# The last three of 39 expert blocks behind a test of the routing

## The chip, the cores and the metric

The kernel runs on one core of a Trainium2 chip. The core has five engines with an instruction stream each: TensorE (PE, matmuls; its weight loads are listed as PEld), VectorE (DVE), ScalarE (ACT), GpSimd (POOL) and SyncE (SP, which issues DMAs). They meet through semaphores. The metric is the device time of one execution in microseconds (us); lower is better. All data is float32.

## The reference

Two transformer-like layers on 8 sequences of 512 tokens with 256 features. In each layer the normalised input goes through a sequence mixer and a mixture of experts, and both results are added to the input. In the first layer the mixer is a state-space model in both directions, and the experts are these:

```python
logits = xt @ Wr + br                    # xt: 4096 tokens x 256, 8 experts
probs = softmax(logits)
gate = max(probs);  idx = argmax(probs)  # one expert for each token
h1 = maximum(xt @ W1[idx] + b1[idx], 0)  # 256 -> 1024
y = (h1 @ W2[idx] + b2[idx]) * gate      # 1024 -> 256
```

How many tokens an expert gets depends on the data. The second layer is an attention with 16 heads and a decay over the distance, and a mixture of experts with a fixed capacity; it needs the whole first layer of a sequence before it can begin on it.

## The kernel before, in words

**First layer, mixer.** The work is cut into 8 batches (one sequence each, 512 tokens) of 8 chunks (4 stretches of 128 tokens, each in two directions), 64 chunks in all. The order of every engine's instructions is written out by hand. A loop over the chunks issues, for each chunk, the state-space steps (`segments`, the exponentials of `cross`, `inside`, `before`, `pairs`, `behind`, `weigh`) and pieces of the neighbouring batches (`project`, `conv`, `z_part`, `output`). The first exponential of a chunk is on line 1111, the matmuls of `segments` on 1103, those of the projections on 915.

**Fills.** Between these the loop calls `fill(1)`, four times a chunk, five times in the first two chunks of a batch and in the last twelve chunks. One fill takes one step of a generator: first `rows`, which is `route0()` followed by `blocks()`, and when that has ended `rest`, which is `late()`. After the last chunk the steps of the last batch are issued with more fills between them, and what is left of `late` goes into the first steps of the second layer's attention.

**Routing.** `route0` (lines 472 to 528) finds the expert of each token and sorts the tokens into blocks of 128 of one expert each. An expert with n tokens gets n/128 blocks, rounded up. `end` holds the running sum of these, so its last entry is the number of blocks in use. In the worst case this is `NBLK` = (4096 + 8 x 127)/128, rounded down to 39, and the kernel always runs 39. A block behind the last one in use gathers rows of zeros, loads the weights of the last expert, and scatters its result to rows out of bounds, which are dropped.

**Blocks.** For each block GpSimd issues four indirect DMAs: a gather of the 128 token rows (`xd`, line 581), the two weight matrices of the expert (`w1`, `w2`, line 586, about 1 MB each), fetched up to two blocks ahead, and the scatter of the result (`put`, line 609). PE turns the rows (line 601), multiplies by `w1` (line 634) and `w2` (line 655); ScalarE and VectorE take half each of the activation (641, 643); ScalarE scales the bias (627) and VectorE combines (661). A block is five steps, so five fills.

**Late work.** `late` loads the second layer's weights into the space that the blocks' tiles leave (`second_weights`, lines 72 and 845 to 874; the release waits for the last scatter), and then runs, for each batch as its first layer is done, its normalisation (`norm`, lines 679 to 725), transposition and projections (`turn`, `project`, lines 737 to 744 and 246 to 280) and the second router (`route`, with matmuls on line 226). The three run side by side, one step of each in a fill.

The lines that set this order:

```python
rows, rest, sizes = itertools.chain(route0(), blocks()), late(), step_sizes()
...
def fill(n):
    for _ in range(n):
        if next(rows, "end") == "end":
            next(rest, None)
```

Of the kernel before, what the change touches and what calls it, by code (L numbers as in the profile page):

```python
# [32 lines left out]
NE, FF = 8, 1024  # L33
FC = FF // P
NBLK = (NT + NE * (P - 1)) // P
CAP = NT // NE
NE1 = NE - 1
NSLOT1 = NE1 * CAP
# [21 lines left out]
def tile_kernel(ctx: ExitStack, tc: tile.TileContext, t, out: bass.AP):  # L60
# [299 lines left out]
    number0 = l0c.tile([P, NBLK], I32, name="number0", tag="number0")  # L360
    ea = l0c.tile([P, 2 * NH], FP, name="ea", tag="ea")
    w_idx = l0c.tile([P, NBLK], I32, name="w_idx", tag="w_idx")

    dec_tok = l0c.tile([P, 2, NTILE, NH], FP, name="dec_tok", tag="dec_tok")

# [106 lines left out]
    def route0():  # L472

        big = r0b

        E3 = [P, NTILE, NE]
        pair0 = big.tile([P, NTILE, 2], FP, name="pair0", tag="pair0")
        G.iota(
            pair0[:, :, 0], pattern=[[P, NTILE]], base=1, channel_multiplier=1, allow_small_or_imprecise_dtypes=True
        )  # L480
        for pr in softmax_experts(big, proj[:, :, 2 * NH :], br):
            yield
        m, oh = first_max(big, pr, "a")
        V.tensor_copy(pair0[:, :, 1], m)
        yield
        rank, n = ranks(
            big, lambda name, shape: bank(name, shape, "e"), oh,
            lambda shape: row("rk_b").rearrange("p (a b) -> p a b", a=2),
        )
        yield  # L490
        over = big.tile([P, NE, NTILE], FP, name="over", tag="over")
        V.tensor_tensor(over, bc(n, 2, [P, NE, NTILE]), bc(iota_t, 1, [P, NE, NTILE]), ALU.is_gt)
        nb = big.tile([P, NE], FP, name="nb", tag="nb")
        V.tensor_reduce(nb, over, AX.X, ALU.add)
        end = big.tile([P, NE], FP, name="end", tag="end")
        V.tensor_copy(end, nb)
        for e in range(1, NE):
            V.tensor_tensor(end[:, e : e + 1], end[:, e : e + 1], end[:, e - 1 : e], ALU.add)
        yield
        first = big.tile([P, NE], FP, name="first", tag="first")  # L500
        V.tensor_tensor(first, end, nb, ALU.subtract)
        V.tensor_scalar(first, first, float(P), None, ALU.mult)
        V.tensor_tensor(rank, rank, bc(first, 1, E3), ALU.add)
        lo, hi = (big.tile([P, NTILE], FP, name=n, tag=n) for n in ("lc_l", "lc_h"))
        locate(big, slots_of(big, oh, rank, "a"), lo, hi)
        yield

        tp, n, entry = bank("tab", [P, NBLK, 2], "e"), TPB, None
        for i in range(0, NTILE + n, n):
            at = slice(i, i + n)  # L510
            ahead = entries(big, NBLK, lo[:, at], hi[:, at], pair0[:, at, :]) if i < NTILE else None
            if entry:
                enter(tp, entry, i == n, i == NTILE)
            entry = ahead
            yield
        V.tensor_copy(table0, tp)
        numbers(big, table0, number0)

        B3 = [P, NBLK, NE - 1]
        iota_b = big.tile([P, NBLK], FP, name="iota_b", tag="iota_b")  # L520
        G.iota(iota_b, pattern=[[1, NBLK]], base=0, channel_multiplier=0, allow_small_or_imprecise_dtypes=True)
        past = big.tile(B3, FP, name="past", tag="past")
        V.tensor_tensor(past, bc(end[:, : NE - 1], 1, B3), bc(iota_b, 2, B3), ALU.is_le)
        be = big.tile([P, NBLK], FP, name="be", tag="be")
        V.tensor_reduce(be, past, AX.X, ALU.add)
        V.tensor_scalar(be, be, float(P), pidx, ALU.mult, ALU.add)
        V.tensor_copy(w_idx, be)
        yield

    def decays():  # L530
# [33 lines left out]
    with ExitStack() as es:  # L564
# [9 lines left out]
        def fetch(j, *names):  # L574

            if j < NBLK:
                for name in names:
                    n, bufs = {"xd": (DM, 3), "w1": (KC * FF, 2), "w2": (FC * DM + FC + DM, 2)}[name]
                    w = held[name, j] = e2.tile([P, n], FP, name=name, tag=name, bufs=bufs)
                    if name == "xd":  # L580
                        G.indirect_dma_start(
                            out=w, out_offset=None, in_=xn0, bounds_check=NT + P - 1, oob_is_err=True,
                            in_offset=bass.IndirectOffsetOnAxis(ap=number0[:, j : j + 1], axis=0),
                        )
                    else:
                        G.indirect_dma_start(
                            out=w, out_offset=None, in_=t[name], bounds_check=NE * P - 1, oob_is_err=False,
                            in_offset=bass.IndirectOffsetOnAxis(ap=w_idx[:, j : j + 1], axis=0),
                        )
# [3 lines left out]
        def blocks():  # L593
            nonlocal e2
            r0.close()
            e2 = es.enter_context(tc.tile_pool(name="e2", bufs=2, side="right"))
            def turned(j):
                xd = held.pop(("xd", j))
                tp = bank("xdT_ps", [P, DM], "e")
                for k in range(KC):  # L600
                    T.transpose(tp[:, k * P : (k + 1) * P], xd[:, k * P : (k + 1) * P], ident)
                xdT = e2.tile([P, DM], FP, name="xdT", tag="xdT", bufs=3)
                A.copy(xdT, tp)
                return xdT

            sent = []

            def put(yo, number):
                one = G.indirect_dma_start(
                    out=yt0, out_offset=bass.IndirectOffsetOnAxis(ap=number, axis=0),  # L610
                    in_=yo, in_offset=None, bounds_check=NT - 1, oob_is_err=False,
                )
                for other in sent:
                    tc.declare_no_dep(one.ins, other.ins, reason="every token has one row")
                sent.append(one)

            made = None
            fetch(0, "xd", "w1", "w2")
            fetch(1, "xd", "w1", "w2")
            yield  # L620
            nxt = turned(0)
            yield
            for j in range(NBLK):
                xdT, (w1, w2) = nxt, (held.pop((name, j)) for name in ("w1", "w2"))
                b12 = w2[:, FC * DM :]
                yo = e2.tile([P, DM], FP, name="yo", tag="yo")
                A.mul(yo, b12[:, FC:], table0[:, j, 1:2])
                hT = [e2.tile([P, FC // 2, P], FP, name="hT", tag="hT", bufs=2) for _ in range(2)]
                for half in range(2):
                    hp = bank("h_ps", [P, FC // 2, P], "e")  # L630
                    for i in range(FC // 2):
                        f = half * FC // 2 + i
                        for k in range(KC):
                            T.matmul(  # L634
                                hp[:, i, :], w1[:, k * FF + f * P : k * FF + (f + 1) * P],
                                xdT[:, k * P : (k + 1) * P], start=(k == 0), stop=(k == KC - 1),
                            )
                    for i in range(FC // 2):
                        f = half * FC // 2 + i
                        if half == 0:  # L640
                            A.activation(hT[half][:, i, :], hp[:, i, :], AF.Relu, bias=b12[:, f : f + 1])
                        else:
                            V.tensor_scalar(hT[half][:, i, :], hp[:, i, :], b12[:, f : f + 1], 0.0, ALU.add, ALU.max)
                    if half == 0 and j:
                        put(*made)
                        fetch(j + 1, "w2")
                    if half == 0:
                        fetch(j + 2, "xd")
                    yield
                if j + 1 < NBLK:  # L650
                    nxt = turned(j + 1)
                    yield
                yp = bank("y_ps", [P, DM], "e")
                for f in range(FC):
                    T.matmul(  # L655
                        yp, hT[f // 4][:, f % 4, :], w2[:, f * DM : (f + 1) * DM], start=(f == 0), stop=(f == FC - 1)
                    )
                    if f == 3:
                        fetch(j + 2, "w1")
                        yield  # L660
                V.scalar_tensor_tensor(yo, yp, table0[:, j, 1:2], yo, ALU.mult, ALU.add)
                made = yo, number0[:, j : j + 1]
                yield
            put(*made)

        kept, turned = {}, set()

# [1173 lines left out]
```

## Time and profile before

| | |
|---|---|
| median of 3 runs | 2013.36 us (2012.37 to 2015.62) |
| the profiled execution | 2011.26 us |
| its span, first to last instruction | 2009.5 us |
| mean granted clock of TensorE | 0.943 of full speed |
| TensorE busy | 1818.5 us, 90% of the span |
| VectorE, ScalarE, GpSimd busy | 1459.0, 1176.2, 587.2 us |
| first and last block's closing VectorE step (line 661) | 220.4 and 878.4 us |
| first score matmul of the second layer (line 1533) | 1128.7 us |

The profile is of one execution. A group's line names the source line, the engine and operation, the tile written and those read, the shape, and the count; then busy us and mean ns of one, and then the time that the engine stood idle before these instructions, with what ended it. A matmul in float32 leaves two records for each call. "Issue" is time in which the engine waited for nothing that the profile shows. A row of busy time by stage gives each engine's busy us within a stretch of the span, then the granted clock of TensorE as a fraction and what the DMA engines did.

### The profile page before, as it was taken

Reading aid. Unit: us, or ns where it says so; the run is one execution under the profiler, and the core shown is the slowest. Engines: PE = TensorE matmul, PEld = TensorE weight load, DVE = VectorE, ACT = ScalarE, POOL = GpSimd, SP = SyncE. Lnnn points to the kernel's source line nnn. Section 1 sums busy time; section 2 is a strip of 40 time slices with the busy share of each in tenths; the row PEclk is TensorE's granted clock in tenths of the full one; section 3 lists DMA queues with packets and bytes.
Section 4 is the critical chain, followed back from the end, with each engine's and each line's share of the span. In section 5 each row is a group of like instructions: output and inputs, shape, how many; then the busy total and the mean of one; then the engine's idle time right before and its main releaser. Section 6 shows DMA issues by size and latency. Waiting matters only on the chain.

```text
span 2009.5 us, 33675 instructions
## 1 busy us (share of the span) xinstructions
PE 1818.5 (90%) x11956; PEld 1239.9 (62%) x11956; DVE 1459.0 (73%) x3344; ACT 1176.2 (59%) x2575; POOL 587.2 (29%) x528
## 2 busy tenths in 40 slices
PE   6566999899999999998898869999999999999997
PEld 6224677676767767664565546666666666666654
DVE  6587675767667576778557477878888878788885
ACT  4232454434545454454552337878887887788886
POOL 0042665655556574543330000101011111111030
PEclk8677999999999999998898679999999999999999
DMA  7010565545556554436553313222313222223171
GB/s 267 6 47 26 211 212 171 180 143 172 197 171 206 170 189 160 161 104 172 154 165 93 98 44 108 66 84 57 89 49 103 66 85 54 87 57 100 40 143 42
DMA packets 132967, 238.58 MB, mean 119 GB/s; under 512 B 20381, under 2 KB 94111, under 8 KB 120896
## 3 DMA queue, kind: packets, MB, share of 16 engines
q1 hardware_dynamic: 101952, 119.99, 19.1%
q0 software_dynamic: 29808, 115.78, 18.7%
q8 instruction: 96, 1.57, 0.3%
q10 hardware_dynamic: 1040, 0.66, 0.1%
q14 instruction: 71, 0.58, 0.1%
HBM read 183.58 MB, written 53.71 MB: 118 GB/s over the span
## 4 chain that ended last, share of the span: by engine, by line
PE 66%; DVE 14%; ACT 11%; issue 2%; DMA 1%; POOL 0%; SPq 0%; ACTq 0%; DVEq 0%; POOLq 0%
PE p_ps L1555 8%; PE h_ps L634 6%; PE pj L915 6%; PE y_ps L655 6%; ACT s L1548 6%; PE o_ps L1564 6%; PE s_ps L1533 4%; PE e_hp L1383 4%; PE e_yp L1396 4%; ACT pT L1556 3%; PE op L1060 3%; PE yd L1141 3%; PE seg L1103 2%; PE sp L1171 2%; PE yoff L1159 2%
## 5 line engine op out<-in xcount | busy, mean ns | idle before, releaser
L1538 DVE TENSOR_SCALAR s<-s_ps 128x512 f32<-128x512 f32 x512 | 318.0, 684 | 137.2 <-PE s_ps L1533 135.5
L1548 ACT ACTIVATE s<-s,ng 128x512 f32<-128x512 f32 x512 | 330.9, 717 | 10.9 <-DVE ng L1544 10.9
L1540 DVE CUSTOM_DVE_ANT_0 s<-s,band 128x512 f32<-128x512 f32 x512 | 323.1, 689 | 0.0
L1556 ACT COPY pT<-p_ps 128x512 f32<-128x512 f32 x512 | 276.0, 588 | 65.1 <-PE p_ps L1555 57.1
L1555 PE MATMUL p_ps<-ident,s 128*128 128x128 f32 x2048 | 285.7, 283 | 21.1 <-ACT pT L1556 15.0
L1555 PEld LDWEIGHTS p_ps<-ident,s 128*128 128x128 f32 x2048 | 236.1, 144 | 95.5 <-ACT pT L1556 31.7
L1403 POOL DMA_INDIRECT x<-e_yo,number x28 | 45.9, 1639 | 626.8 <-ACT e_yo L1402 620.8
L915 PE MATMUL pj<-xT,w_w_in 128*128 128x512 f32 x384 | 201.1, 650 | 12.7 <-DVE cv L928 6.6
L634 PEld LDWEIGHTS h_ps<-xdT,w 128*128 128x128 f32 x1248 | 151.7, 195 | 20.6 <-issue 19.8
L1533 PE MATMUL s_ps<-kT,qT 16*128 16x512 f32 x1024 | 157.4, 659 | 5.3 <-DMA kT<-kd 2.2
L928 DVE SCALAR_TENSOR_TENSOR cv<-pj,w_conv_w,cv 128x511 f32<-128x511 f32 (+2 forms) x192 | 143.3, 747 | 22.7 <-ACT cv L924 18.2
L634 PE MATMUL h_ps<-xdT,w 128*128 128x128 f32 x1248 | 155.0, 279 | 0.1
L655 PE MATMUL y_ps<-w,hT 128*128 128x256 f32 x624 | 147.7, 380 | 0.0
L1087 POOL TENSOR_TENSOR au<-da,half 128x512 f32<-128x512 f32 x64 | 78.4, 1225 | 202.8 <-PE seg L1103 131.7
L655 PEld LDWEIGHTS y_ps<-w,hT 128*128 128x128 f32 x624 | 115.7, 190 | 32.4 <-issue 17.1
L1383 PE MATMUL e_hp<-e_xdT,e_w 128*128 128x256 f32 x448 | 121.5, 394 | 10.9 <-ACT e_hT L1386 8.8
L915 PEld LDWEIGHTS pj<-xT,w_w_in 128*128 128x128 f32 x384 | 71.1, 203 | 96.0 <-issue 81.1
L1564 PE MATMUL o_ps<-pT,vt 128*32 128x256 f32 x2048 | 126.8, 386 | 0.0
L1150 DVE TENSOR_TENSOR yT<-yT,yd 128x512 f32<-128x512 f32 (+1 forms) x64 | 43.8, 684 | 98.8 <-PE yd L1141 98.3
L1396 PE MATMUL e_yp<-e_w,e_hT 128*128 128x256 f32 x448 | 113.3, 385 | 0.2 <-ACT e_hT L1386 0.2
L1564 PEld LDWEIGHTS o_ps<-pT,vt 128*32 128x32 f32 x2048 | 61.1, 111 | 83.0 <-issue 49.6
L1116 ACT ACTIVATE mt<-seg,mid 64x64 f32<-64x64 f32 x512 | 109.4, 309 | 0.7
(326 smaller groups left out, 3033.4 us busy)
## 6 DMA issues: line engine op xcount, KB each, us to landing
ex<-exd SPq DMA_DIRECT2D x96, 128.0 KB
fr<-fdd SPq DMA_DIRECT2D x64, 128.0 KB
od<-os SPq DMA_DIRECT2D x28, 256.0 KB
e_w<-in_ei_dram SPq DMA_DIRECT2D x7, 1024.0 KB
e_w<-in_eo_dram SPq DMA_DIRECT2D x7, 1024.0 KB
vd<-vt SPq DMA_DIRECT2D x16, 288.0 KB
vt<-vd SPq DMA_DIRECT2D x8, 576.0 KB
u<-in_u_dram SPq DMA_DIRECT2D x8, 512.0 KB
```

What stands on the lines that cost most here:

```text
L634: T.matmul(hp[:, i, :], w1[:, k * FF + f * P : k * FF + (f + 1) * P], xdT[:, k * P : (k + 1) * P], start=(k == 0), stop=(k == KC - 1),)
L655: T.matmul(yp, hT[f // 4][:, f % 4, :], w2[:, f * DM : (f + 1) * DM], start=(f == 0), stop=(f == FC - 1))
L915: T.matmul(pj, w_in[:, k, o * P : (o + 1) * P], self.xT[:, k, :], start=(k == 0), stop=(k == KC - 1))
L1383: T.matmul(hp, w1[:, k, f * P : (f + 1) * P], xdT[:, k, :], start=(k == 0), stop=(k == KC - 1))
L1396: T.matmul(yp, hT[:, f, c * P : (c + 1) * P], w2[:, f, :], start=(f == 0), stop=(f == FC - 1))
L1533: T.matmul(sp[i], self.q[r, cols], self.k[r, :], start=True, stop=True)
L1538: V.tensor_scalar(self.p[i], sp[i], -CLAMP, CLAMP, ALU.max, ALU.min)
L1540: V.tensor_tensor_reduce(out=self.p[i], in0=self.p[i], in1=band[:, at : at + S], scale=1.0, scalar=-3.0e38, op0=ALU.mult, op1=ALU.max, acc ...
L1548: A.activation(self.p[i], self.p[i], AF.Exp, bias=self.ng[:, i : i + 1])
L1555: T.transpose(pp[:, k, :], self.p[i][:, k * P : (k + 1) * P], ident)
L1556: A.copy(pT[i][:, :, cc * P : (cc + 1) * P], pp)
L1564: T.matmul(op[32 * i : 32 * i + 32, half * 2 * P : (half + 1) * 2 * P], self.v[:, k, h * (AD + 1) : h * (AD + 1) + 32], pT[i][:, k, :], st ...
```

## The change

The loop of `blocks` becomes a generator `run(lo, hi)`. `run(0, 36)` is issued as before, step by step between the chunks. The number of blocks in use is copied by VectorE into a tile `many` at the end of `route0`; at the start of `blocks` all five engines load it into a register, which takes a fill of its own. When `run(0, 36)` has ended, all of `run(36, 39)` is issued in one go within `tc.If(used > 36)`: a part of each engine's stream that the engine skips when the test fails. Within a run nothing is fetched past its end, so the part has its own first fetches and its own first turn, and its last scatter. Steps of other work can't be put between its own.

```diff
+OFTEN = NBLK - 3
...
+    many = l0c.tile([P, 1], I32, name="many", tag="many")
...
         V.tensor_copy(w_idx, be)
+        V.tensor_copy(many, end[:, NE - 1 :])
         yield
...
-            made = None
-            fetch(0, "xd", "w1", "w2")
-            fetch(1, "xd", "w1", "w2")
-            yield
-            nxt = turned(0)
-            yield
-            for j in range(NBLK):
+            def run(lo, hi):
+
+                made = None
+                for j in range(lo, min(lo + 2, hi)):
+                    fetch(j, "xd", "w1", "w2")
+                yield
+                nxt = turned(lo)
+                yield
+                for j in range(lo, hi):
...
-                    if half == 0 and j:
-                        put(*made)
-                        fetch(j + 1, "w2")
-                    if half == 0:
-                        fetch(j + 2, "xd")
+                        if half == 0 and j > lo:
+                            put(*made)
+                            if j + 1 < hi:
+                                fetch(j + 1, "w2")
+                        if half == 0 and j + 2 < hi:
+                            fetch(j + 2, "xd")
...
-                if j + 1 < NBLK:
-                    nxt = turned(j + 1)
-                    yield
+                    if j + 1 < hi:
+                        nxt = turned(j + 1)
+                        yield
...
-                        fetch(j + 2, "w1")
-                        yield
+                            if j + 2 < hi:
+                                fetch(j + 2, "w1")
+                            yield
...
-            put(*made)
+                put(*made)
+
+            used = nc.values_load(many[0:1, 0:1], engines=list(ENGINES), min_val=0, max_val=NBLK)
+            yield
+            yield from run(0, OFTEN)
+            with tc.If(used > OFTEN):
+                for _ in run(OFTEN, NBLK):
+                    pass
+            yield
```

The lines that are not shown are the same as before, one level further in.

More of the change, by code (lines that the diff above doesn't have):

```diff
@@ L615, in put @@
                 sent.append(one)
-            made = None
-            fetch(0, "xd", "w1", "w2")
-            fetch(1, "xd", "w1", "w2")
+            def run(lo, hi):
[6 more added lines that the diff above has]
+                for j in range(lo, hi):
+                    xdT, (w1, w2) = nxt, (held.pop((name, j)) for name in ("w1", "w2"))
+                    b12 = w2[:, FC * DM :]
+                    yo = e2.tile([P, DM], FP, name="yo", tag="yo")
+                    A.mul(yo, b12[:, FC:], table0[:, j, 1:2])
+                    hT = [e2.tile([P, FC // 2, P], FP, name="hT", tag="hT", bufs=2) for _ in range(2)]
+                    for half in range(2):
+                        hp = bank("h_ps", [P, FC // 2, P], "e")
+                        for i in range(FC // 2):
+                            f = half * FC // 2 + i
+                            for k in range(KC):
+                                T.matmul(
+                                    hp[:, i, :], w1[:, k * FF + f * P : k * FF + (f + 1) * P],
+                                    xdT[:, k * P : (k + 1) * P], start=(k == 0), stop=(k == KC - 1),
+                                )
+                        for i in range(FC // 2):
+                            f = half * FC // 2 + i
+                            if half == 0:
+                                A.activation(hT[half][:, i, :], hp[:, i, :], AF.Relu, bias=b12[:, f : f + 1])
+                            else:
+                                V.tensor_scalar(
+                                    hT[half][:, i, :], hp[:, i, :], b12[:, f : f + 1], 0.0, ALU.add, ALU.max
+                                )
+                        if half == 0 and j > lo:
[8 more added lines that the diff above has]
+                        yield
+                    yp = bank("y_ps", [P, DM], "e")
+                    for f in range(FC):
+                        T.matmul(
+                            yp, hT[f // 4][:, f % 4, :], w2[:, f * DM : (f + 1) * DM],
+                            start=(f == 0), stop=(f == FC - 1),
+                        )
+                        if f == 3:
+                            if j + 2 < hi:
+                                fetch(j + 2, "w1")
+                            yield
+                    V.scalar_tensor_tensor(yo, yp, table0[:, j, 1:2], yo, ALU.mult, ALU.add)
+                    made = yo, number0[:, j : j + 1]
+                    yield
+                put(*made)
@@ L620, in blocks @@
+            used = nc.values_load(many[0:1, 0:1], engines=list(ENGINES), min_val=0, max_val=NBLK)
             yield
-            nxt = turned(0)
+            yield from run(0, OFTEN)
+            with tc.If(used > OFTEN):
+                for _ in run(OFTEN, NBLK):
+                    pass
             yield
-            for j in range(NBLK):
[L624 to L639, printed above, removed]
-                        if half == 0:
-                            A.activation(hT[half][:, i, :], hp[:, i, :], AF.Relu, bias=b12[:, f : f + 1])
-                        else:
-                            V.tensor_scalar(hT[half][:, i, :], hp[:, i, :], b12[:, f : f + 1], 0.0, ALU.add, ALU.max)
-                    if half == 0 and j:
-                        put(*made)
-                        fetch(j + 1, "w2")
-                    if half == 0:
-                        fetch(j + 2, "xd")
-                    yield
-                if j + 1 < NBLK:
-                    nxt = turned(j + 1)
-                    yield
[L653 to L658, printed above, removed]
-                        fetch(j + 2, "w1")
-                        yield
-                V.scalar_tensor_tensor(yo, yp, table0[:, j, 1:2], yo, ALU.mult, ALU.add)
-                made = yo, number0[:, j : j + 1]
-                yield
```

## The prediction

> **What bounds the kernel now.** I read the page's busy shares first, then the groups by line for what one block costs, then busy time by stage (stretches cut at events of the timeline), then the waits and the timeline at the two places where the change adds something.
>
> The page's head: TensorE (PE) is the busiest engine; instructions come in 16 KB packets.
>
> ```profile
> span 2009.5 us, 33675 instructions
> PE 1818.5 (90%) x11956; PEld 1239.9 (62%) x11956; DVE 1459.0 (73%) x3344; ACT 1176.2 (59%) x2575; POOL 587.2 (29%) x528
> ...
> q8 instruction: 96, 1.57, 0.3%
> ```
>
> Groups by line: the parts of a block, each over all 39 blocks.
>
> ```profile
> L634 PE MATMUL h_ps<-xdT,w 128*128 128x128 f32 x1248 | 155.0, 279 | 0.1
> L655 PE MATMUL y_ps<-w,hT 128*128 128x256 f32 x624 | 147.7, 380 | 0.0
> L601 PE MATMUL xdT_ps<-ident,xd 128*128 128x128 f32 x78 | 15.3, 278 | 6.0 <-DVE mt L1135 6.0
> L586 POOL DMA_INDIRECT w<-in_w_dram,w_idx x78 | 87.2, 1118 | 22.9 <-issue 16.1 <-PE cb L1124 2.3 <-PE h_ps L634 1.7
> L609 POOL DMA_INDIRECT yt<-yo,number x39 | 44.1, 1130 | 52.2 <-DVE yo L661 47.8 <-issue 4.4
> ```
>
> Busy time by stage. Columns: stretch, length, then busy us of PE, its weight loads, VectorE, ScalarE, GpSimd, the granted clock, DMA share, GB/s.
>
> ```profile
> 268.00:834.80 566.80, 554.04 (x3333) 400.36 (x3332) 371.40 (x646) 265.37 (x743) 313.37 (x275) 0.99 0.52 177
> 834.80:878.40 43.60, 43.35 (x274) 31.15 (x272) 33.21 (x50) 24.71 (x69) 26.85 (x23) 1.00 0.37 119
> 912.40:987.60 75.20, 60.36 (x281) 34.67 (x283) 58.20 (x128) 38.02 (x93) 26.34 (x22) 0.84 0.52 143
> 987.60:1048.20 60.60, 59.61 (x331) 38.62 (x327) 31.42 (x85) 33.35 (x87) 20.92 (x20) 0.97 0.64 189
> 1068.50:1108.00 39.50, 34.16 (x161) 23.89 (x161) 27.20 (x93) 7.87 (x14) 2.52 (x3) 0.75 0.25 69
> 1108.00:1125.40 17.40, 17.40 (x83) 12.88 (x82) 3.80 (x13) 4.40 (x8) 0.00 (x0) 0.89 0.15 54
> ```
>
> To be seen: while blocks fill the chunks, PE is busy 98 to 99% of the time at full clock, and 834.8 to 878.4 is the stretch of blocks 36 to 38 (from the last VectorE step L661 of block 35 to that of 38). So PE time removed there is time. Behind the last chunk (1068.5 on) PE runs at 0.75 of its clock: that tail is late work between the last batch's own steps.
>
> Timeline, where the counts become known, and a wait of SP:
>
> ```profile
> 192.09 1.13 PE L1103 MATMUL seg<-au,row_lt 64*128 64x512 f32 x4
> ...
> 194.82 0.18 DVE L527 CAST w_idx<-be 128x39 int32<-128x39 f32 x1
> ...
> 199.26 0.66 PE L601 MATMUL xdT_ps<-ident,xd 128*128 128x128 f32 x2 [6.04 <-DVE mt L1135]
> ```
> ```profile
> SPq L72 <- DMA yt<-yo,number: 28.9, 1, 28.9
> ```
>
> PE has 6.04 us to spare there; and SP already stands 28.9 us for the landing of the last block's rows before it loads the second layer's weights.
>
> **Is the conditional part run?** Working the router's formula on the reference's inputs, the experts get 595, 493, 659, 443, 659, 357, 362 and 528 tokens, that is 5+4+6+4+6+3+3+5 = 36 blocks of 128. The test is "more than 36", so the part is skipped; no count is within 15 tokens of a block's edge.
>
> **The change, part by part.** The sum is made against the profiled execution, 2011.26 us (span 2009.5 and 1.8 around it). It stands 2.1 below the median of the three runs, 2013.36, which I add back at the end.
>
> 1. Three blocks less. PE for one: 155.0/39 + 147.7/39 + 15.3/39 = 3.97 + 3.79 + 0.39 = 8.15 us; three are 24.5. The weight loads lie beside the matmuls. ScalarE loses (19.6 + 44.3 + 14.4)/39 x 3 = 6.0 us and VectorE (43.9 + 18.8)/39 x 3 = 4.8; both have a quarter or more of this stage free, so I count nothing. GpSimd issues 12 indirect DMAs less (six of L586, three of L581, three of L609): 6.7 + 3.5 + 3.4 = 13.6 us of an engine that is 55% busy here, counted as nothing; the traffic, some 7 MB of weights, ran at a DMA share of 0.37 to 0.52. -24.5.
>
> 2. Late work moves up. A fill runs one step of the blocks or, when these are through, of the second layer's preparation (norm, turn, project, route). Blocks had 2 + 39 x 5 - 1 = 196 steps; now 1 + 2 + 36 x 5 - 1 + 1 = 183. So the late work starts 13 fills, or some three chunks of 14.9 us (268.0 to 879.5 over 41 chunks), earlier: with it its SP loads (L72, L679), stores (L701, L725, L256) and GpSimd's L682, all past the same queue's ex and fr loads. SP's stop before L72 stays, at its new place. The 13 steps put into the loop are, by place, those that now run from 1068.5 to 1108: 30.0 of its 34.2 us of PE (L226 11.5, L261 5.6, L279 4.1, L270 2.3, L744 2.1 and smaller). At full clock this is 30.0 x 0.75 = 22.5. +22.5. Late steps leave PE waiting on VectorE: from 912.4 to 1048.2 PE is idle 14.8 + 1.0 = 15.8 us over 45 fills, 0.35 each, times 13: +4.6.
>
> 3. The tail shrinks. From 1068.5 to 1125.4 are 56.9 us. The last batch's own chain is four gate steps of 0.68, a square of 0.63, its sums 1.06 and 0.58, the means 1.05, a reciprocal root of 3.3 and outputs (2.91 + 1.99 + 1.89 + 1.99 = 8.8): 18.2. Beside it stays the turn of batch 6, some 11.9 us of PE (L737, L744, L246, L261, L270, L279). 56.9 - 30.1 = 26.8, -27. Batch 6 is ready only at chunk 61 and its norm takes 13 fills, so its turn gains about 10 fills, not 13: three steps at 39.5/13 = 3.0 us stay in the tail in place of 1.7 in the loop: +4.
>
> Parts 1 to 3: -24.5 + 22.5 + 4.6 - 27 + 4 = -20.4.
>
> 4. The copy of the count on VectorE: as L527, 0.18 us, in PE's idle stretch: 0. One more fill before the first fetch is in the 183.
>
> 5. The register load on five engines. It waits for VectorE's copy at about 195.0. Behind it stand, on PE the segments L1103 (192.09) with 6.04 us of idle to cover it; on ScalarE the exponentials L1111 (197.97), which wait for L1103; on VectorE, behind the weighing that ends at 198.96, the scaling L1309; on GpSimd the first fetch, which waits for VectorE anyway; on SP the ex loads. The trace has no such load: below are the register moves of 29 ns, above a chunk of lookahead lost, 14.9. A load waits on memory and not on other engines, so I take 1.0, what ScalarE and VectorE can't hide; without PE's cover it would be some 3 more.
>
> 6. The conditional, after block 35. Five engines test and jump, and semaphores must be brought to the counts that later waits expect. Nothing in the trace shows this. Below: a few semaphore instructions of 17 to 51 ns, 0.1 us (no gain: it only adds). Above: all engines stop until the slowest is through, 14.9. Nearest rows: the landing of a block's rows, 2.3 us (issue 879.19, released 881.49), which GpSimd may have to await, and one instruction packet, 0.3% of 16 engines' 2009.5 us over 96, so 1.0 us. I take 4.0, near these rows. Behind it on PE stands the chunk's own work; ScalarE and VectorE wait for that.
>
> [...]
>
> 7. PE's clock. After an idle of 2.99 us the four matmuls L915 at 918.30 took 3.78 us, at 912.30 without it 1.98; with L1159 behind them (1.91 against 1.06) 2.7 us were lost. A stop of part 6 may cause this: half of it, 1.4.
>
> Sum: -20.4 + 1.0 + 4.0 + 1.4 = -14.0; 2011.3 - 14.0 = 1997.3, and with 2.1 back 1999.4.
>
> **Rivals.**
> A: cheap and wholly overlapped. Parts 5 to 7 cost 0.5 in all, and the loop takes the late steps without the 4.6 and the 4: 2013.4 - 29.0 + 0.5 = 1984.9; half of these two held, 1989. For it: PE's 6.04 us of cover. Against it: 0.84 of the clock from 912 to 988.
> B: no change. The late steps do not fit: VectorE is busy 77% from 912.4 to 987.6, and if the tail gives back only half of 27, parts 1 to 3 are -6.9, and with 6.4 the time is 2013. Against it: from 987.6 PE is 98% busy with late work.
> C, slower: both added places (195 and about 838 us) stop all five engines until their queues are empty, and each costs a chunk of lookahead: 29.8 - 20.4 = +9.4, 2023. It decides from 10.2 us a stop. For it: engines run far apart (SP 28.9 us ahead). Against it: a load and a test need no other engine.
> D: the part is run after all: its three blocks alone, without chunks between, at least 3 x 8.15 us of PE and the waits of one block's chain; over 2030.
>
> **How the numbers follow.** My sum 0.50 (its own range 1990 to 2009), A 0.17, B 0.10, C 0.21, D 0.02. The predicted time is 1999. Within 0.2% (4 us, about what a measurement of this kernel can tell from no change) is B; faster are my sum and A, 0.67; slower C and D, 0.23. The range, 1984 to 2024, takes in A and most of C and leaves out the upper part of C and D.
>
> **What would show it.** L634 x1152, L655 x576, L586 x72, L609 x36: skipped. SP's first second-layer load (881.6) some 45 us earlier; the first scores of the second layer (L1533, 1128.7) at about 1115. Part 5 is wrong if chunk 4's exponentials come more than 2 us after 197.97; part 6 if any engine stands over 5 us where the blocks end; part 3 if 1068.5 to 1125.4 keeps over 40 us. The prediction falls if the two stops together reach 18 us, or if the loop stretches by what the tail gives.

## The result, and the profile after

The changed kernel takes 2001.5 us (median of ten executions, 1993.9 to 2007.4) against 2014.9 us for the kernel before (ten beside it, 2010.7 to 2030.4). The ratio is 0.9923 with a 95% interval of 0.9902 to 0.9943, so 15.5 us less, give or take 4 (the two medians differ by 13.4). The forecast was 1999. The profiled execution took 1997.8 us (span 1995.9), 3.7 below the median; that of before, 2011.26, is 3.6 below its own. The two spans differ by 13.6 us, and the forecast's sum was 14.0.

The head of the page of the changed kernel:

```profile
span 1995.9 us, 33334 instructions
PE 1792.2 (90%) x11806; PEld 1214.1 (61%) x11806; DVE 1457.8 (73%) x3330; ACT 1170.0 (59%) x2557; POOL 572.7 (29%) x516
...
q8 instruction: 96, 1.57, 0.3%
```

Groups by line of the changed kernel (busy us, mean ns, idle before):

```profile
L639 PE MATMUL h_ps<-xdT,w 128*128 128x128 f32 x1152 | 142.0, 277 | 1.9 <-DMA w<-in_w_dram,w_idx 1.9
L663 PE MATMUL y_ps<-w,hT 128*128 128x256 f32 x576 | 138.7, 385 | 0.0
L604 PE MATMUL xdT_ps<-ident,xd 128*128 128x128 f32 x72 | 14.0, 277 | 0.0
L589 POOL DMA_INDIRECT w<-in_w_dram,w_idx x72 | 80.9, 1123 | 22.0 <-issue 14.1 <-PE cb L1142 2.3 <-PE h_ps L639 2.0
L612 POOL DMA_INDIRECT yt<-yo,number x36 | 41.5, 1152 | 39.2 <-DVE yo L671 35.1 <-issue 3.4 <-DVE yT L1049 0.3
```

Exactly 36 blocks are run: 150 matmul records are missing, and PE is busy 26.3 us less. The instruction queue moves 96 packets as before, so the skip saves none of those.

To see where the 13.6 us come from I cut both traces at events that all kernels have: the weighing step (line 1135 before, 1153 after) of the chunks numbered 47, 51 and 62 in the timeline (the first that it shows being 0), and the first scores of the second layer. Blocks end around the first cut. Busy time in these three stretches (length, then PE, its weight loads, VectorE, ScalarE, GpSimd, the granted clock, DMA share, GB/s), first the kernel before, then the changed one with its block stage ahead:

```profile
838.60:890.40 51.80, 49.92 (x306) 34.13 (x303) 38.43 (x68) 28.90 (x81) 31.60 (x33) 1.00 0.40 127
890.40:1047.00 156.60, 139.27 (x720) 85.56 (x718) 106.73 (x245) 81.29 (x206) 56.04 (x50) 0.91 0.56 156
1047.00:1128.70 81.70, 70.51 (x357) 48.85 (x355) 48.43 (x158) 23.52 (x49) 4.40 (x5) 0.85 0.33 95
```
```profile
268.00:837.30 569.30, 559.83 (x3367) 403.75 (x3366) 374.03 (x652) 266.53 (x746) 313.27 (x275) 0.99 0.52 172
...
841.20:889.80 48.60, 35.32 (x181) 19.26 (x182) 39.18 (x76) 27.85 (x70) 27.63 (x29) 0.89 0.55 135
889.80:1062.30 172.50, 155.15 (x792) 93.01 (x790) 118.55 (x282) 82.73 (x211) 53.02 (x49) 0.91 0.46 133
1062.30:1117.20 54.90, 48.27 (x274) 33.70 (x270) 33.19 (x97) 17.55 (x37) 4.09 (x4) 0.95 0.43 123
```

I call the three stretches S1, S2 and S3. Up to S1 the changed kernel is 2.6 us late; then S1 is 3.2 shorter, S2 15.9 longer, S3 (the tail) 26.8 shorter, and the second layer 2.1 shorter (880.8 against 878.7). Together 13.6. The gain is in the tail, and the loop gives about half of it back. S1 hardly shrank, although before it held most of the three blocks (132 of their 150 matmul records, 21.8 of their 24.5 us of PE; the rest lies just ahead of it): PE has 14.6 us less to do there but stands still for 13.3 us in place of 1.9, and its clock fell from 1.00 to 0.89.

The first added place. Timeline, and the register load by its source line (durations min/median/max ns, start in us):

```profile
191.70 0.14 DVE L530 CAST many<-end 128x1 int32<-128x1 f32 x1
192.59 1.28 PE L1121 MATMUL seg<-au,row_lt 64*128 64x512 f32 x4 [3.65 <-DVE cv L946]
195.37 0.60 ACT L1129 ACTIVATE mt<-seg 128x512 f32<-128x512 f32 x1 [0.58 <-issue]
```
```profile
L676 SPq TENSOR_LOAD <-many x1: 482/482/482, 191.9 to 191.9; - x1
L676 PEldq TENSOR_LOAD <-many x1: 493/493/493, 191.9 to 191.9; - x1
L676 DVEq TENSOR_LOAD <-many x1: 542/542/542, 193.3 to 193.3; - x1
L676 ACTq TENSOR_LOAD <-many x1: 477/477/477, 194.2 to 194.2; - x1
```

Each engine spends about half a microsecond (GpSimd, not shown, 497 ns). Chunk 4's exponentials start at 195.37, against 197.97 before; but the changed kernel is already 2.9 us ahead at its first weighing (122.54 against 125.43), well before the load. Counted from there they start 0.3 us later.

The second added place, the conditional, by its source line, and who waited on the timeline:

```profile
L679 SPq COMPARE_BRANCH  x1: 53/53/53, 827.3 to 827.3; - x1
L679 PEldq COMPARE_BRANCH  x1: 3317/3317/3317, 835.4 to 835.4; - x1
L679 POOLq COMPARE_BRANCH  x1: 53/53/53, 837.9 to 837.9; - x1
L679 DVEq COMPARE_BRANCH  x1: 72/72/72, 840.5 to 840.5; - x1
L679 ACTq COMPARE_BRANCH  x1: 45/45/45, 841.4 to 841.4; - x1
L679 POOLq INC_SWDGE_SEM  x1: 937/937/937, 841.9 to 841.9; - x1
```
```profile
839.31 1.13 PE L1121 MATMUL seg<-au,row_gt 64*128 64x512 f32 x4 [0.30 <-PEq L679]
...
842.52 1.09 PE L1159 MATMUL yd<-mt,xdt 128*64 128x128 f32 x16 [0.51 <-DVEq L679]
842.99 1.18 POOL L1105 TENSOR_TENSOR au<-da,half 128x512 f32<-128x512 f32 x1 [3.69 <-DMA yt<-yo,number]
```

The engines jump one after the other over 14 us, each when it gets there: no common stop. The longest jump is PE's, 3.3 us, issued while matmuls were still queued (PE ran them from 835.40 to 839.01 us), so that PE itself waited 0.30 us for it. GpSimd waited 3.69 us, as part 6 named it, for the landing of the last block's rows.

### The profile page after: what moved, and what is told of

It is laid out like the page before. It is cut to its first block, busy times and chain, and to the rows that moved or that the text cites. A ratio compares the mean times of both kernels' runs of the same rounds, so it can differ in the third digit from the quotient of the medians.

```text
span 1995.9 us, 33334 instructions
## 1 busy us (share of the span) xinstructions
PE 1792.2 (90%) x11806; PEld 1214.1 (61%) x11806; DVE 1457.8 (73%) x3330; ACT 1170.0 (59%) x2557; POOL 572.7 (29%) x516
## 4 chain that ended last, share of the span: by engine, by line
PE 67%; DVE 16%; ACT 12%; issue 3%; DMA 2%; POOL 0%; SPq 0%; ACTq 0%; DVEq 0%; POOLq 0%
PE p_ps L1573 8%; PE pj L933 7%; PE h_ps L639 6%; ACT s L1566 6%; PE o_ps L1582 6%; PE y_ps L663 6%; PE e_hp L1401 5%; PE s_ps L1551 4%; PE e_yp L1414 4%; ACT pT L1574 3%; DVE cv L946 3%; PE yd L1159 3%; PE seg L1121 3%; PE op L1078 2%; PE sp L1189 2%
## 5 line engine op out<-in xcount | busy, mean ns | idle before, releaser
L639 PEld LDWEIGHTS h_ps<-xdT,w 128*128 128x128 f32 x1152 | 138.9, 194 | 20.4 <-issue 19.6
L639 PE MATMUL h_ps<-xdT,w 128*128 128x128 f32 x1152 | 142.0, 277 | 1.9 <-DMA w<-in_w_dram,w_idx 1.9
L663 PE MATMUL y_ps<-w,hT 128*128 128x256 f32 x576 | 138.7, 385 | 0.0
L663 PEld LDWEIGHTS y_ps<-w,hT 128*128 128x128 f32 x576 | 108.3, 193 | 29.9 <-issue 16.1
```

The costliest lines, as they stand in the source:

```text
L639: T.matmul(hp[:, i, :], w1[:, k * FF + f * P : k * FF + (f + 1) * P], xdT[:, k * P : (k + 1) * P], start=(k == 0), stop=(k == KC - 1),)
L663: T.matmul(yp, hT[f // 4][:, f % 4, :], w2[:, f * DM : (f + 1) * DM], start=(f == 0), stop=(f == FC - 1),)
```

## The experiments

All times stand against the kernel before, run beside them; the stretches are from the one profiled execution of each. An execution's granted clock and its time go together: over 83 executions of the kernel before, 0.001 of mean clock goes with 1.05 us (a straight line through them, 2.9 us of scatter around it). So a profile's tail can be 10 us off the median's (an estimate: e10's profiled execution has a clock of 0.929, its median 0.938), which matters below.

| kernel | ratio to before, 95% | S1, us | S2, us | S3, us |
|---|---|---|---|---|
| before | 1 | 51.8 | 156.6 | 81.7 |
| changed | 0.9923 [0.9902, 0.9943] | 48.6 | 172.5 | 54.9 |
| e1, no load, no test | 0.9924 [0.9903, 0.9945] | 47.3 | 174.6 | 53.7 |
| e3, 13 empty fills | 0.9942 [0.9921, 0.9962] | 41.0 | 160.5 | 84.0 |
| e4, one block conditional | 1.0016 [1.0001, 1.0030] | 49.8 | 157.9 | 89.4 |
| e5, nothing removed | 1.0045 [1.0020, 1.0069] | 53.4 | 160.1 | 83.0 |
| e13, e5 again | 1.0019 [1.0000, 1.0037] | 53.3 | 160.2 | 83.6 |
| e11, load only | 1.0022 [1.0008, 1.0037] | 51.8 | 158.9 | 82.6 |
| e12, load and real test | 1.0030 [1.0011, 1.0049] | 53.4 | 159.2 | 83.4 |
| e2, body always run | 1.0081 [1.0052, 1.0109] | 83.5 | 168.3 | 61.2 |
| e6, matmuls of 50 us | 1.0145 [1.0106, 1.0184] | 74.6 | 158.4 | 81.9 |
| e10, matmuls of 25 us | 1.0041 [1.0016, 1.0065] | 52.6 | 158.4 | 93.0 |
| e7, denser fills | 0.9911 [0.9879, 0.9943] | 48.9 | 169.0 | 61.4 |
| e8, sparser fills | 0.9968 [0.9942, 0.9994] | 49.1 | 158.7 | 77.4 |

**e1: no load and no test.** The changed kernel without the copy of the count, the load and the conditional part: 36 blocks, with the fills in the same places. It computes the right thing only where 36 blocks suffice, as here.

```
-        V.tensor_copy(many, end[:, NE - 1 :])
...
-            used = nc.values_load(many[0:1, 0:1], ...)
             yield
             yield from run(0, OFTEN)
-            with tc.If(used > OFTEN):
-                for _ in run(OFTEN, NBLK):
-                    pass
             yield
```

> 36 blocks as in the changed kernel and the same number of fills, but without the count's copy, the register loads and the test; the last three blocks are not in the program at all. If the conditional and the load cost the 6.4 us of my parts 5 to 7, this is 6.4 us faster than the changed kernel, about 1995 us (ratio to before 0.989 to 0.990). Rival, read from the trace of the changed kernel (loads of 0.5 us on each engine, PE's 3.3 us branch hidden behind its queued matmuls, GpSimd's 3.7 us wait hidden): within 2 us of the changed kernel, 1999 to 2002, ratio about 0.993.

Measured: 1998.8 us, a ratio of 0.9924 beside 0.9923. The load and the test make no difference that this can tell (each interval is 4 us to either side). Where they stand, S1 is 1.3 us shorter without them. The loop's stretch is there all the same: S2 is 174.6 us. So neither of the two is what stretches it.

**e3: the late work stays at its old fills.** Thirteen empty steps behind the conditional part.

```
             with tc.If(used > OFTEN):
                 for _ in run(OFTEN, NBLK):
                     pass
             yield
+            for _ in range(13):
+                yield
```

> The changed kernel with 13 empty fills behind the conditional part, so that the late work starts at its old fill. If the gain is the blocks' PE time given back partly in the loop, the three chunks concerned fall from 14.5 to the 10 us that chunks 50 and 51 took with little late work in the kernel before, some 9 to 12 us less in the loop, and the tail keeps its old length (68 us from chunk 62's weighing to the first scores): 2002 to 2006. Rival: the gain comes only from the late work starting earlier, the blocks' own time is not on the path: 2010 to 2014.

Measured: 2003.5 us, 0.9942. Windows of this kernel, S1 to S3:

```profile
839.00:880.00 41.00, 33.12 (x168) 17.46 (x168) 34.29 (x53) 24.10 (x64) 24.53 (x26) 0.88 0.27 73
880.00:1040.50 160.50, 141.32 (x722) 86.27 (x720) 107.31 (x245) 81.36 (x206) 56.28 (x50) 0.90 0.55 152
1040.50:1124.50 84.00, 72.63 (x356) 51.04 (x355) 48.49 (x158) 23.44 (x49) 4.47 (x5) 0.81 0.32 93
```

This splits the change in two. Blocks gone and nothing in their place: S1 is 10.8 us shorter than before, not 24.5. Against before's first line, PE is busy 16.8 us less (49.92 to 33.12: the 168 records left run at 0.88 of the clock) and idle 6.0 us more (1.88 to 7.88); 16.8 - 6.0 = 10.8. S2 and S3 then come out 3.9 and 2.3 longer with the same PE records: in S3 PE is busy 2.1 us more at a lower clock (0.81 against 0.85), in S2 busy 2.0 more (0.90 against 0.91) and idle 1.9 more. The second part, late work moved up 13 fills, is the changed kernel against this one: S1 + 7.6, S2 + 12.0, S3 - 29.1, so 19.6 us into the loop and 29.1 out of the tail. By the times, three blocks gone are worth 11.7 us (0.0058 of 2014.5), give or take 4, and the move 3.8 more, with some 6 to either side. The stretches, one execution of each, split the same gain as 4.6 and 9.5 (below); e3's execution had a mean clock of 0.938 where the changed kernel's had 0.946. How the gain divides between the two is therefore known to some 6 us only, and a gain of the move alone is not shown by these two kernels' times.

**e6 and e10: only the blocks' matmuls put back.** e3's empty fills issue matmuls on data that is already there; nothing reads the results. e10 is half of e6.

```
+            for part in range(13):
+                hp = bank("h_ps", [P, FC // 2, P], "e")
+                for i in range(FC // 2):
+                    for k in range(2):            # e10: once
+                        T.matmul(hp[:, i, :], ident, ident, ...)
+                yp = bank("y_ps", [P, DM], "e")
+                for f in range(4):                # e10: 2
+                    T.matmul(yp, ident, w_in[:, 0, :DM], ...)
+                yield
```

> The changed kernel, and behind the conditional part 13 more fills that issue only matmuls of the blocks' shapes on data that is already there (104 of 128x128 and 52 of 128x256, about 25 us of PE at full clock, against 24.5 for three blocks); no fetch, no activation, no put, and nothing reads the results. The late steps start where they did before the change. Against the 13 empty fills (2003.5, -11 to before). Theory 1 (it was the PE time of the three blocks that was worth 11 us, the rest of the 24.5 having been lost to an idle PE and its lower clock): the time returns to that of the kernel before, 2011 to 2017, chunks 48 to 51 take again some 52 us in place of 41, and the granted clock from 839 to 876 is 1.0 again in place of 0.84 to 0.90. Theory 2 (the gain came from what else a block holds, its indirect transfers, GpSimd and ScalarE steps): the time stays within 4 us of 2003.5.

> As the kernel with only matmuls put in for the blocks, with half as many: that kernel's 13 fills held 208 matmuls of 128x128 and 104 of 128x256 as the profile counts them, 50.0 us of PE and not the 25 that I had stated. Here it is 104 and 52, 25 us, as three blocks have 24.5. Theory 1 (PE time is what the blocks cost there): with 50 us the time was 45 us over that of 13 empty fills (0.9942 to before), so the first 5 to 14 us fall into time that PE has free; with 25 us I expect +11 to +20, a ratio of 0.9995 to 1.004, and a granted clock of 0.97 or more from 839 to 876. Theory 2 (other parts of a block are worth the gain of 13 empty fills): each us of PE costs 0.9 from the first one on, +22, a ratio of 1.005 or more, or, if PE were free here, within 4 us of 0.9942.

My count for e6 was wrong by two: each matmul in the code is two in the profile, and the 13 fills held 50.0 us of PE. Measured: e6 2048.4 us (1.0145), e10 2020.9 (1.0041, just past the 1.004 of theory 1, with an interval that also takes in the 1.005 of theory 2; the trace decides). Their S1:

```profile
841.00:915.60 74.60, 73.79 (x480) 57.84 (x480) 30.93 (x52) 24.20 (x64) 22.34 (x26) 1.00 0.17 41
```
```profile
843.20:895.80 52.60, 51.15 (x324) 36.34 (x324) 32.09 (x52) 24.26 (x64) 23.52 (x26) 1.00 0.22 57
```

With 0, 25 and 50 us of matmuls S1 is 41.0, 52.6 and 74.6 us long: the first 25 us cost 11.6, the next 25 cost 22.0. And the clock in S1 is 0.88, 1.00 and 1.00. So matmuls alone bring back all that the blocks' removal had saved in S1 (11.6 against 10.8), without their transfers, activations and GpSimd steps, and they bring the full clock back. This carries the reading of e3: of the 21.8 us of PE taken out of S1, 11.0 brought nothing, because the chunks' own steps, left alone, kept PE waiting (7.9 of e3's 41.0 us) and its clock low (0.88). In run times e10 stands 20 us above e3 and not 11.6. Its executions had lower clocks (median 0.938 against 0.942): at equal clock, by the line above, e10 is 2.9 us over the executions of before beside it and e3 10.2 under its own, so 13 us apart. In its profile the rest is in the tail (S3 93.0 at a clock of 0.72) and the second layer; the section on the hardware shows how.

**e4, e5, e11, e12, e13: what the load and the test cost.** e4 makes only the last block conditional (OFTEN = NBLK - 1). The others run all 39 blocks unconditionally at the old fills:

```
             used = nc.values_load(many[0:1, 0:1], ...)
-            yield
-            yield from run(0, OFTEN)
-            with tc.If(used > OFTEN):
+            yield from run(0, NBLK)
+            with tc.If(used > NBLK):      # e5, e13; e12: used > OFTEN; e11: no If
                 for _ in run(OFTEN, NBLK):
                     pass
-            yield
```

> The test at 38, so only the last block stands in the conditional part and 38 run. My sum: a third of -20.4 and the whole 6.4 of the stops, -0.4, no change (2013). Rival, stops of 1 us or so: about -4 to -5, 2009. [...]

> All 39 blocks run as in the kernel before, at the same fills; the register load stands in the first fetch's fill and behind the last block a conditional part of three blocks whose test (more than 39) never holds. Nothing is removed, so this is the price of load and test alone: +6.4 us by my sum (2020, ratio 1.003), 0 to +2 by the reading of the trace, +20 or more if the engines had to stop together.

> All 39 blocks at their old fills, with the copy of the count and the register load on five engines, and no conditional part. Theory 1 (the load costs nothing, the 9 us of the kernel that had load and an empty test come from its executions at a lower clock or from the test): ratio 0.998 to 1.002. Theory 2 (the load costs some 8 us): 1.004 or more.

> All 39 blocks at their old fills, then the test that the changed kernel has (more than 36), with a body of three further blocks that is jumped over. In the earlier kernel of this kind the test was against 39, and its trace shows no COMPARE_BRANCH, only the semaphores brought to their counts. Theory 1 (load and conditional cost under 4 us): ratio 0.998 to 1.002, a COMPARE_BRANCH of some 3.3 us on PE's load queue that lies behind queued matmuls, PE waiting under 1 us. Theory 2 (they cost the 6.4 us of the prediction or more): 1.003 to 1.007.

> The kernel with all blocks, load and a test that can never hold, run again beside the two above. Theory 1 (its +9 us were lower clocks of some of its executions, 0.929 to 0.934 where the others had 0.940): this time within 5 us of the kernel before, 0.998 to 1.0025. Theory 2 (something in it costs 9 us): 1.0045 again.

Measured: e4 2017.4 us, so one block less (and three late steps earlier) gains nothing, and neither of its two forecasts (2013 and 2009) came; its S1 is 2.0 us shorter for 8.15 us of PE, and its one profile has a long tail (S3 89.4, also in the section on the hardware). e5 2023.7 (+9), e13, the same again, 2018.1 (+4), e11 2018.8 (+4), e12 2019.1 (+6, between 2 and 10): by its time at the lower edge of theory 2 (1.003), and e11 just past theory 1 (1.002). In e11 the load stayed on SP alone (481 ns; e12 has one on each of the five engines); the other engines only waited for the count.

In place the traces agree closely. S1 of e11, then of e12:

```profile
833.20:885.00 51.80, 49.91 (x306) 34.12 (x303) 38.53 (x68) 28.60 (x81) 31.60 (x33) 1.00 0.40 127
```
```profile
832.80:886.20 53.40, 50.17 (x306) 34.20 (x303) 38.44 (x68) 28.87 (x81) 31.49 (x33) 1.00 0.39 124
```

S1 is 51.8 us in e11, as before, and 53.4, 53.4 and 53.3 in the three kernels with a conditional part. **The conditional costs 1.6 us where it stands** (1.3 by e1). The jump on PE, in e4 and then e12:

```profile
L679 PEldq COMPARE_BRANCH  x1: 228/228/228, 857.2 to 857.2; - x1
```
```profile
L678 PEldq COMPARE_BRANCH  x1: 454/454/454, 868.7 to 868.7; - x1
```

For the load no place shows a cost: from the first to the seventh weighing of the timeline before took 101.1 us, e12 101.1, e11 103.1, e1 without the load 103.2, the changed kernel 105.5. The twelve kernels with the load (e11's on SP alone) spread from 101.1 to 106.1 here, with a mean of 104.1, against 101.1 and 103.2 for the two without it; its cost lies within that spread, at most a few us, and is not settled closer.

That leaves some 2 to 4 us of the 4 to 6 in e11, e12 and e13 that no row shows. These executions have lower granted clocks (medians 0.938 to 0.9415, against 0.9445 beside them); compared at equal clock by the line above they are 0.5, 1.6 and 0.6 us over the kernel before, and e5 0.6 (2.8 over the executions beside it, which lie 2.1 under the line). Whether the added code makes the clock lower or these executions happened to have it, the runs do not tell. e5's 9 us did not come again: e13's interval ends at 1.0037, as its theory 1 had it.

**e2: the part is run after all.** The test becomes one that always holds, and all 39 blocks are computed.

```
-            with tc.If(used > OFTEN):
+            with tc.If(used > 0):
```

> The test is changed to one that always holds, so blocks 36 to 38 are run inside the conditional part. They are then built in one piece, between two chunks, with no chunk's work between their steps, and all 39 blocks are computed. Theory 1 (what the part costs is the chain of one block: fetch, turn, matmuls, activation, second matmuls, put, each waiting for the one before): the first fetch alone is about 2.3 us of landing and more for the weights of 0.5 MB each, then three blocks at 8.15 us of PE that nothing else covers; I expect some 15 us of filling the chain and 3 x 10 to 12, so +40 to +50 over the changed kernel, 2040 to 2050, a stretch of 40 us or more between the weighing steps of chunks 47 and 48 in place of some 12. Theory 2 (PE alone counts): +24.5, about 2026.

Measured: 2037.5 us, 1.0081: by the ratio 16 us over before (20 by the medians) and 32 over the changed kernel, between the two theories. PE's timeline there:

```profile
837.55 0.69 PE L604 MATMUL xdT_ps<-ident,xd 128*128 128x128 f32 x2 [3.52 <-DMA xd<-xn,number]
841.86 6.28 PE L639 MATMUL h_ps<-xdT,w 128*128 128x128 f32 x32 [3.62 <-DMA w<-in_w_dram,w_idx]
847.98 0.38 PE L604 MATMUL xdT_ps<-ident,xd 128*128 128x128 f32 x2
849.36 3.72 PE L663 MATMUL y_ps<-w,hT 128*128 128x256 f32 x16 [1.00 <-DVE hT L648]
852.92 3.73 PE L639 MATMUL h_ps<-xdT,w 128*128 128x128 f32 x32
...
860.89 3.73 PE L639 MATMUL h_ps<-xdT,w 128*128 128x128 f32 x32
864.46 3.62 PE L663 MATMUL y_ps<-w,hT 128*128 128x256 f32 x16
868.01 1.13 PE L1121 MATMUL seg<-au,row_gt 64*128 64x512 f32 x4
```

The three blocks take from 834.0, where PE falls idle, to 868.0. Only the first pays for its chain: 7.1 us of waiting for its transfers, and its first matmuls take 6.28 us in place of 3.73. Then the blocks overlap each other (852.92 to 860.89 is 8 us, PE's own time for a block), which is what I had missed in theory 1. This is about the price where a routing needs 37 to 39 blocks; no run had such a routing.

**e7 and e8: more or fewer late steps in the loop.** A chunk's fifth fill starts 16 or 8 chunks from the end in place of 12.

```
-                if n % 8 < 2 or n >= N - 12:
+                if n % 8 < 2 or n >= N - 16:     # e7;  e8: N - 8
```

> The changed kernel with the fifth fill of a chunk from the last 16 chunks on in place of the last 12: four more late steps lie in the loop, and the tail has four less. Theory 1 (each late step costs in the loop what it saves in the tail, as 22 against 29 us over 13 steps say, about 0.5 us gained a step): 1998 to 2002, no difference that the runs can tell. Theory 2 (chunks 48 to 51 have PE idle for 11 of 36 us, so that steps put there cost nothing): the tail's 4 x 2.2 us are gained, 1991 to 1994.

> The changed kernel with the fifth fill of a chunk only in the last 8 chunks in place of the last 12: four late steps less in the loop, four more in the tail. Theory 1 (a step costs about the same at both places): 2000 to 2004. Theory 2 (steps in the loop are free, those in the tail are not): 2008 to 2011. Theory 3 (the loop is crowded, its late steps are what stretched it by 24 us in all): 1992 to 1996.

Chunks 48 and 49, as the first two of a batch, have their fifth fill in any case, so e7 moves two steps (of chunks 50 and 51) and not the four of its expectation; e8 moves four. Measured: e7 2001.0 us, 0.9911; e8 2013.0, 0.9968. e7's interval overlaps that of the changed kernel, so no gain is shown; but two free steps would have gained only some 4 us, less than the runs can tell here, so e7 does not decide between its theories. e8 loses 9 us of the 15.5, give or take 7 (theory 2's place: 0.9968 of 2014.5 is 2008). Against the changed kernel its loop is 13.3 us shorter (S1 + S2, 207.8 against 221.1) and its tail 22.5 longer: by these two profiles a step costs 5.6 us in the tail and 3.3 in the loop, and four times the difference is the 9 us. These prices of a step are rough, since they hold the clock of one execution each (0.79 in e8's tail, 0.95 in the changed kernel's): e7's profile, with two steps more in the loop, has a loop 3.2 us shorter and a tail 6.5 longer, its tail at 0.76. "The loop is crowded" (theory 3) falls by e8's time: taking late steps out of the loop lost time. No version tried is shown to beat the changed kernel.

## Why the prediction was right

The time (1999 forecast, 2001.5 measured) and the direction were right. Term 1 was twice too large; terms 2, 3 and 6 erred the other way and made up for it. That the total came out within 3 us is luck: one of the sum's largest terms failed, and others happened to fail against it.

1. **Three blocks less, -24.5: the step that failed.** It said that PE time removed there is time, because PE was busy 98 to 99% while blocks fill the chunks. That row describes chunks with blocks. Without blocks the same chunks have PE idle and at 0.88 of the clock (e3's S1): -10.8 in place for the 21.8 us that went from there, some -12 in the run times, e10's matmuls giving the same 11.6 back. A full engine shows that its work is not hidden; it does not show what bounds the stretch once that work is gone.
2. **Late work into the loop, +22.5 + 4.6 = +27.1:** measured +19.6 (changed kernel against e3, one profile each). Some of it fell into the time that the missing blocks had left idle in S1, +7.6 for the first of the steps. Both terms seem mis-sized from one cause: I had counted the free time as gain in term 1 and the late steps at full price in term 2.
3. **The tail, -27 + 4 = -23:** measured -29.1 against e3 and -26.8 against before. Tail steps also hold waits and low clock, which go with them: PE idle 11.4 us there in e3 and 6.6 in the changed kernel, at 0.81 and 0.95 of the clock. Cut as the prediction cut it, from the last chunk to the last output, the tail fell from 58.8 us (1066.6 to 1125.4) to 20.9 (1091.6 to 1112.5), where 30 were forecast to stay.

   Parts 1 to 3 together were -20.4. By the same stretches they are 41.0 - 51.8 + 3.9 + 2.3 = -4.6 for the blocks and 19.6 - 29.1 = -9.5 for the move, -14.1, with the conditional's 1.6 inside. With 2.6 ahead of S1 and -2.1 in the second layer they make the 13.6. The 2.6 is traced to nothing: from the first weighing to S1 the kernels of this document take between 709 and 719 us, with no order that the changes explain.
4. **The copy of the count, 0:** 0.14 us on VectorE ahead of PE's idle stretch; right.
5. **The register load, 1.0:** half a microsecond on each engine (477 to 542 ns, begun at 191.9 on three of them, at 193.3 and at 194.2 us on the others), exponentials not late; nothing here contradicts it, but its price is not settled closer than a few us.
6. **The conditional, 4.0:** measured 1.6 (e11 against e5, e12, e13) and 1.3 (e1). It had the right pieces, the landing that GpSimd waits for (3.69 us) and a jump on PE (3.3 us, against 0.05 to 0.07 on the other engines), but the engines meet them one after another (827.3 to 841.4 us), with chunk work queued. A jump over the same body took PE 0.45 us in e12, so the body alone does not give the price. The 3.3 us cost PE 0.30 us, as the jump lay behind queued matmuls.
7. **Half clock after a stop, 1.4:** PE had no stop over 0.51 us at the conditional, and its clock read 1.00 from 837.3 to 845. Wrong as placed.

The rivals. **A** (1985 to 1989) was right that the stops cost little in place, and wrong that the three blocks give their full time. **B** had its mechanism, since the loop does stretch (S1 + S2 by 12.7), but the tail gave all of its 27. **C** falls: e12 holds both added places with nothing removed and costs 6 us (2 to 10), not 29.8. **D** did not happen, and e2 prices it at 2037.5. Of the signals, the counts, parts 3 and 5 and the first scores (1117.2, promised about 1115) came as stated. At the conditional no engine stood over 3.7 us; GpSimd did stand 8.9 us just ahead of it, for VectorE's step of the chunk (L1182), but in the kernel before, too, it stands over 5 us 17 times between 268 and 880 us, so that wait is not put down to the conditional. SP's first second-layer load came at 850.7, 31 us earlier and not 45: SP stood 22.7 us behind its jump for PE's step L1026, which its next store (L928) needed.

## What to carry to other kernels

Before counting removed work at its full duration on the busiest engine, ask what that engine would do in its place: here 24.5 us of matmuls were worth some 11, because the steps around them did not keep PE fed on their own (idle 7.9 of 41.0 us in e3). Their place was then worth filling with later work (e8, four steps fewer there, lost 9 us, give or take 7), and such work has to be priced at both ends: what it adds where it goes, and what it takes from where it was. A skipped part cost 1.6 us in its place here; put it where every engine has work queued (PE's jump of 3.3 us then cost it 0.30), and know the price when it does run (16 us over the loop without a test).

## What the runs showed of the hardware

**The clock stayed at half for 14 to 43 us while PE was busy.** In e10's profile, a 3.94 us wait in the tail is followed by some 43 us at exactly half the clock, although PE is then nearly always busy. Windows of e10, and the wait on its timeline:

```profile
1085.00:1100.00 15.00, 12.30 (x34) 8.18 (x34) 8.68 (x26) 3.97 (x7) 0.00 (x0) 0.50 0.22 48
1100.00:1115.00 15.00, 14.28 (x55) 10.67 (x55) 6.44 (x17) 1.75 (x3) 0.00 (x0) 0.50 0.14 49
1115.00:1130.00 15.00, 14.32 (x50) 11.85 (x50) 3.64 (x18) 2.34 (x4) 0.00 (x0) 0.50 0.11 41
```
```profile
1087.70 3.78 PE L262 MATMUL qp<-xT,w_w_q 128*128 128x512 f32 x4 [3.94 <-DVE proj L775]
```

It is not the only one, and another came without a long wait. In e4's tail, PE is busy 88% of the 8 us ahead, with no wait over 0.6 us, and then runs 27.3 us at half the clock without a gap:

```profile
1076.00:1084.00 8.00, 7.05 (x44) 5.21 (x44) 6.99 (x18) 1.41 (x3) 0.00 (x0) 1.00 0.32 88
1084.10:1111.40 27.30, 27.30 (x104) 20.86 (x104) 8.80 (x30) 5.63 (x11) 0.00 (x0) 0.50 0.12 42
```

e7's tail has 27.3 us of the same (1062.0 to 1089.3, PE busy 97%), and the kernel before 13.7 (1098.1 to 1111.8, 95%). In e10, too, half the clock is on record from 1082.9, 0.9 us before the wait began. What starts and ends these stretches the runs do not show.

Half the clock for 43 us is some 20 us lost against the full clock (an estimate: 43 x 0.5); the prediction priced a stop at 2.7. It is a likely cause of the spread of these kernels' times (e10's from 2014 at a clock of 0.945 to 2038 at 0.929), but only one execution of each kernel was profiled, so this is not shown.

**The same skip took PE 0.45 or over 3.3 us, by its place.** The body of three blocks was jumped in 3317 ns in the changed kernel, and in 3317 to 3886 ns in the five others that jump it behind block 36 (e3, e6, e7, e8, e10); in e12, behind block 39, in 454 ns; one block (e4) in 228 ns. So it is no chance of one execution. What it is about the place, the runs do not show. Other engines took 45 to 72 ns. Where the test can never hold (e5), no branch was recorded, but the waits were: GpSimd still waited 2.3 us for the landing of the last rows, and then spent 1.2 us on an instruction INC_SWDGE_SEM.
